# Subtracting a constant from x on ScalarE instead of GpSimd, with another set of due times, in a four-layer graph attention kernel

## The chip, the cores and the metric

The kernel runs on one core of a Trainium2 chip. A core has TensorE for matrix products (its weight loads are listed apart as PEld), VectorE (DVE), ScalarE (ACT), GpSimd (POOL) and SyncE (SP). Each engine takes its own instructions strictly in the order in which they were written for it, and waits at each until what it needs has arrived. SP and POOL issue most of the DMA transfers. The metric is the device time of one execution in microseconds.

## The reference

x has the shape 8 x 2048 x 128 (batch, node, feature), and adj is a symmetric 2048 x 2048 matrix of 0 and 1 with the diagonal set. Four layers follow each other, each of the form x = x + layer(relu(layernorm(x)), adj):

- Layers 0, 1 and 3 are graph attention. With Wh = h W and two scores per node s1 and s2, the weights are softmax over j of leaky_relu(s1[i] + s2[j]), limited to neighbours. Layer 0 ends in elu, layer 1 in nothing. Layer 3 scales its input per node, normalizes Wh a second time, adds Wh as a residual and ends in elu.
- Layer 2 has four heads of 32 features: softmax over j of leaky_relu(x[i] . x[j]), limited to neighbours, applied to x itself.

elu(v) is v for positive v, and exp(v) - 1 otherwise, so elu(v) = min(exp(v), 1) + max(v, 0) - 1. The two elus of a batch element bring a -1 each. A layernorm doesn't change when a constant is added to the whole of its input, so the kernel takes 2 from x once, ahead of the layers, and leaves out both -1.

## The kernel before

**Staging.** `fast` holds the whole adjacency matrix in on-chip memory as bytes (`edge`) and up to four batch elements of x (`X[b]`, 128 partitions x 16 blocks x 128 features, so 2048 numbers per partition). A unit is one layer of one batch element: class `Gat` for layers 0, 1 and 3, `Heads` for layer 2.

**Work of a unit.** `rows_made` normalizes x: VectorE takes statistics (L460), GpSimd raises the variance to -0.5 (`moments_power`, L111), and ScalarE makes the normalized rows (L527; for layer 3 also L534). TensorE transposes them (L558) and projects them (L588). A `Gat` then runs 32 tokens, 16 for each half of the target nodes. For a token, VectorE makes a 128 x 1024 mask of weights (L756), and TensorE multiplies it with the projected rows in eight products (L765, two instructions each). `out` divides, applies elu and adds the result to x, partly by DMA from the POOL queue (L834). A `Heads` runs 64 beats, 16 per head: TensorE makes scores (L1051), ScalarE exponentials of 128 x 1024 (L1058, two per beat), VectorE masks them and sums (L1064), TensorE weighs the values with them (L1073).

**Start.** 16 adjacency rows of 1 MB each are loaded from the SP queue (L368), and VectorE turns each into bytes (L371). `symmetry` and `verdict` establish with TensorE products and ScalarE squares (L385, L389, L395) that the matrix is symmetric, so that `fast` may be used; another path, `general`, follows only if not.

**The subtraction.** `load_x` loads a batch element from the SP queue (L423). For b > 0 its completion isn't given to the layers, but to `less_two` (L430), which adds -2 to the whole of `X[b]` on GpSimd; the statistics of layer 0 need that. For b = 0 the layers start at once, and `less_two(0, ...)` is needed only ahead of the result of layer 0 (`self.less`).

**What sets the order.** The order on the engines is planned while the program is built. Every step is an `Op` with its engine, an assumed duration, a due time, the steps it needs, and the buffers that it takes and frees. `Plan.run` moves through assumed time: of the steps that could start on an engine within WINDOW_US of the first that can, the one with the lowest due time comes next, and is written to that engine's queue. A step that takes a mask buffer (`zg`) counts as HURRY_US earlier while more than one such buffer is free. `Plan` starts with the counts of the buffers, among them `st=2, var=3, norm=3` for the statistics of a layernorm, two pairs of PSUM banks for scores and projections (`pair=(4, 6)`), three `zg` and five `z`.

Due times come from tables: TOKENS gives start and step for each half of a `Gat`, BEATS for each head of a `Heads`, LEADS how long before its start a unit begins. EARLY shifts kinds of steps: a mask's due time is its token's less EARLY["front"], and scores, exponentials, masks and weighings of layer 2 have "score", "exp", "mask" and "sums". `less_two` is due at its load's due time plus 18, and is assumed to last LESS_US, 3.0. The load is assumed to take 0.8 on its queue and 17 more until it has landed. Due times are ranks in a search, not times of the chip.

Of the kernel before, what the change touches and what calls it, by code (L numbers as in the profile page):

```python
# [8 lines left out]
F32 = mybir.dt.float32  # L9
# [5 lines left out]
AF = mybir.ActivationFunctionType  # L15
OP = mybir.AluOpType
# [4 lines left out]
P = 128  # L21
# [19 lines left out]
def adj_preln_d4(ctx: ExitStack, tc: tile.TileContext, x, adj, w0, a0, w1, a1, w3, a3,  # L41
# [17 lines left out]
    nc = tc.nc  # L59
# [8 lines left out]
    const = ctx.enter_context(tc.tile_pool(name="const", bufs=1))  # L68
# [6 lines left out]
    plus_8, minus_8 = plus_8.bitcast(F8), minus_8.bitcast(F8)  # L75
    shift = const.tile([P, 1], F32, name="shift")
    nc.vector.memset(shift, L2_SHIFT)
    neg_half = const.tile([P, NB], F32, name="neg_half")
    nc.vector.memset(neg_half, -0.5)
    edge = const.tile([P, NB, N], U8, name="edge")  # L80
# [75 lines left out]
            self.needs = [n for n in needs if n is not None]  # L156
            self.got, self.end, self.users, self.ready = {}, None, [], 0.0

    HURRY_US, WINDOW_US, BEAT_SUMS_US = 38.6, 0.138, 0.86

    EARLY = dict(front=-419.0, score=436.6, exp=-72.7, mask=-319.1, sums=-351.0)

    SINGLY = (7,)
    FIRST_ALONE = 4
    DIRECT, ROWS_TURNED, L1_ACT, L3_DMA, L3_OUT = ((0, 0), (0, 1), (7, 1), (7, 2)), True, False, True, False
    L3_PLUS, LESS_US = True, 3.0
    PLUS_US, PLUS_LAG_US, GATHER_US, GATHER_LAG_US = 1.0, 5.5, 2.2, 6.5

    class Plan:
# [11 lines left out]
        def add(self, engine, us, due, emit, needs=(), takes=(), frees=(), lag=None, tiled=False):  # L181
            op = Op(engine, us, due, emit, needs, takes, frees, self.LAG[engine] if lag is None else lag, tiled)
            self.ops.append(op)
            return op
# [56 lines left out]
    def fast(ctx):  # L241
# [12 lines left out]
        add = plan.add  # L254
# [161 lines left out]
        X, done = {}, {}  # L416

        def load_x(b, due):
            def load(op):
                X[b] = big.tile([P, NB, C], F32, tag="x", name="x", bufs=4)  # L420
                xv = x[b].rearrange("(n p) c -> p n c", p=P)
                for sl in ([slice(0, NB)] if b else [slice(q * 4, q * 4 + 4) for q in range(4)]):
                    nc.sync.dma_start(out=X[b][:, sl, :], in_=xv[:, sl, :])  # L423

            x_taken[b] = add("SP", 0.8 if b else 2.8, due, load, loaded[:] if b else (), takes=["x"], lag=17.0 if b else 3.5)
            done[b, 0] = [x_taken[b]]
            if b:
                done[b, 0] = [less_two(b, due, done[b, 0])]

        def less_two(b, due, needs):  # L430
            return add("POOL", LESS_US, due + 18.0, lambda op: nc.gpsimd.tensor_scalar(
                X[b], X[b], -2.0, None, op0=OP.add), needs)

        x_taken, behind, y_takers = {}, [], []

# [127 lines left out]
        class Gat(Unit):  # L563
            def beginning(self):
                layer = self.layer
                step = 0.2 if layer != 3 else 0.09
                rhs = {0: rhs0, 1: rhs1, 3: rhs3}[layer]
                made = self.rows_made(0.16, step)
                self.less = [less_two(0, 60.0, [m[1] for m in made])] if (self.b, layer) == (0, 0) else []
                ends, exped, self.v_ready = [], [], []  # L570
                for q in range(4):
# [177 lines left out]
            def token(self, a, due, place, last_front, last_back, first, last, gate=None):  # L749
# [11 lines left out]
                def back(op):  # L761
                    z = self.z.pop(a)
                    for i in range(HB):
# [6 lines left out]
                powers = self.powers if self.layer == 3 else self.r_made[jb // 4]  # L770
                f = add("DVE", 1.2, due - EARLY["front"], front, [last_front, r_ready, rows_in[jb], powers, gate if first else None], takes=["zg"],
                        frees=[("r", taker)] if last else [])
# [156 lines left out]
        class Heads(Unit):  # L929
# [79 lines left out]
            def beats(self, heads):  # L1009
# [4 lines left out]
                for h, (start, step) in enumerate(heads):  # L1014
                    ops = self.load(h, start - 24.0)
                    for jb in range(NB):
# [3 lines left out]
                        for c2 in range(2):  # L1020
                            score = add("PE", 0.455, due - EARLY["score"] + c2, lambda op, s=s, c2=c2: self.scores(op, s, c2),
                                        [score, ops[jb // HB], ops[2]], takes=["pair"] + ["z"] * (c2 == 0))
                            if c2 == 0:
                                z_taker = score
                            exps.append(add("ACT", 1.0, due - EARLY["exp"] + c2, lambda op, s=s, c2=c2, sc=score: self.exp(
                                op, s, c2, sc.got["pair"]), [score], frees=[("pair", score)]))
                        if jb % HB == HB - 1:
                            score.frees.append(("s", ops[jb // HB]))
                        if jb == NB - 1:
                            score.frees.append(("m", ops[4]))  # L1030
                        mask = add("DVE", 2.3, due - EARLY["mask"], lambda op, s=s: self.mask(op, s), [mask] + exps)
                        last.append((z_taker, mask))
                        self.masks.append(mask)
                        if jb % 2 or self.b in SINGLY:
                            n = len(last)
                            weigh = add("PE", BEAT_SUMS_US * n, due - EARLY["sums"], lambda op, s=s, n=n: self.weigh(op, range(s + 1 - n, s + 1)),
                                        [ready, ops[3]] + [m for _, m in last], takes=["low"] * (jb < n),
# [78 lines left out]

        GATES = {(6, 3, 0): (7, 10), (6, 3, 1): (7, 48)}
        TOKENS = {
            (1, 0, 0): (-1045.4, 4.85), (0, 1, 0): (-640.7, 2.76), (0, 1, 1): (-252.6, 5.26),
            (1, 0, 1): (550.0, 6.31), (2, 0, 0): (640.4, 1.65), (2, 0, 1): (28.7, 5.99),  # L1120
            (3, 0, 0): (595.5, 5.24), (1, 1, 0): (-448.5, 2.29), (1, 1, 1): (332.9, 2.97),
            (3, 0, 1): (532.2, 0.52), (2, 1, 0): (784.6, 2.05), (2, 1, 1): (661.4, 2.82),
            (0, 3, 0): (396.7, 5.64), (0, 3, 1): (806.2, 5.15), (3, 1, 0): (813.2, 3.88),
            (3, 1, 1): (626.5, 5.48), (4, 0, 0): (591.3, 5.35), (4, 0, 1): (1159.9, 3.82),
            (1, 3, 0): (344.0, 3.1), (1, 3, 1): (397.9, 2.03), (4, 1, 0): (753.3, 4.65),
            (4, 1, 1): (1047.7, 3.31), (5, 0, 0): (479.5, 5.62), (5, 0, 1): (203.1, 3.96),
            (2, 3, 0): (275.8, 2.82), (2, 3, 1): (1277.7, 3.76), (5, 1, 0): (1267.3, 4.61),
            (5, 1, 1): (1977.2, 2.02), (6, 0, 0): (1682.3, 4.62), (6, 0, 1): (3248.3, 1.23),
            (3, 3, 0): (1175.5, 6.08), (3, 3, 1): (3008.8, 4.11), (6, 1, 0): (2045.9, 2.48),
            (6, 1, 1): (4526.4, 1.12), (7, 0, 0): (2470.3, 4.97), (7, 0, 1): (3262.3, 5.89),  # L1130
            (7, 1, 0): (3469.2, 1.36), (7, 1, 1): (1171.1, 3.15), (4, 3, 0): (4676.8, 5.42),
            (4, 3, 1): (5085.4, 3.02), (5, 3, 0): (4390.1, 5.94), (5, 3, 1): (4885.6, 2.92),
            (6, 3, 0): (2908.7, 3.34), (6, 3, 1): (4037.1, 4.64), (7, 3, 0): (4000.6, 5.22),
            (7, 3, 1): (5814.3, 5.51),
        }
        BEATS = {
            (0, 0): (-220.15, 3.75), (0, 1): (-955.77, 16.21), (0, 2): (-787.01, 14.33),
            (0, 3): (-409.05, 11.49), (1, 0): (-2460.25, 8.82), (1, 1): (-1730.24, 5.06),
            (1, 2): (-1606.84, 2.64), (1, 3): (-953.34, 10.37), (2, 0): (-2913.87, 25.55),
            (2, 1): (-2031.19, 8.77), (2, 2): (-2016.23, 3.56), (2, 3): (-1169.09, 26.22),  # L1140
            (3, 0): (-1338.93, 12.99), (3, 1): (-767.9, 5.05), (3, 2): (-479.82, 24.71),
            (3, 3): (-27.48, 28.61), (4, 0): (-143.12, 33.04), (4, 1): (-664.45, 3.41),
            (4, 2): (334.06, 12.12), (4, 3): (242.61, 6.98), (5, 0): (826.36, 18.62),
            (5, 1): (1257.23, 30.09), (5, 2): (1720.93, 28.28), (5, 3): (2793.45, 29.54),
            (6, 0): (36.7, 6.18), (6, 1): (792.41, 2.76), (6, 2): (1584.95, 2.49),
            (6, 3): (1301.55, 25.56), (7, 0): (-8.2, 11.67), (7, 1): (679.99, 18.73),
            (7, 2): (696.97, 6.2), (7, 3): (1110.52, 5.04),
        }
        LEADS = {
            (0, 0): 213.98, (1, 0): 444.85, (0, 1): 1602.72, (2, 0): 431.88, (1, 1): 877.58,  # L1150
            (3, 0): 3092.27, (2, 1): 1432.74, (0, 3): 1030.57, (3, 1): 74.24, (4, 0): 353.64,
            (1, 3): 11.54, (4, 1): 2797.96, (5, 0): 147.39, (2, 3): 1104.42, (5, 1): 1467.02,
            (6, 0): 886.38, (3, 3): 685.98, (6, 1): 1353.96, (7, 0): 1011.38, (4, 3): 329.93,
            (7, 1): 187.82, (5, 3): 415.04, (6, 3): 2047.57, (7, 3): 660.0, (0, 2): -575.06,
            (1, 2): 1872.75, (2, 2): 1864.09, (3, 2): -603.36, (4, 2): -1021.51, (5, 2): 1002.6,
            (6, 2): -1562.71, (7, 2): 1149.25,
        }

        def planned():
# [217 lines left out]
    with ExitStack() as inner:  # L1377
        inner.enter_context(tc.manual_schedule(engines={
            mybir.EngineType.PE, mybir.EngineType.Activation, mybir.EngineType.DVE,
            mybir.EngineType.Pool, mybir.EngineType.SP}))  # L1380
        fast(inner)
# [28 lines left out]
```

## Time and profile before

| | us |
|---|---|
| median of 3 runs | 2758.52 |
| lowest and highest run | 2756.85, 2759.89 |
| the profiled execution, its own time | 2765.24 |
| its span, from the first to the last instruction | 2763.5 |
| busy: TensorE, VectorE, ScalarE, GpSimd | 2637.1, 2515.8, 1712.1, 331.5 |
| GpSimd in L431, eight times | 45.6 |
| GpSimd in L111, 39 times | 159.1 |

The mean granted TensorE clock is 0.99 of full. Busy time is the time in which an instruction of the engine was under way. In the views, a row of a group has the line in the code, the engine, the operation, the tile written and the tiles read, the shapes and the count; behind the bar come busy time, mean duration in ns, and the idle time ahead of these instructions with what ended it. A row of the waits reads "who waits <- whom: us in total, times, longest". A row of the order of time has start and duration in us; a duration with a count above x1 covers that many instructions in a row.

### The profile page before, as it was taken

How to read it: one execution, taken by the hardware profiler on the slowest of the kernel's cores; microseconds unless marked ns; L12 is line 12 of the kernel's file. 1: busy time of each engine (PE TensorE's matmuls, PEld its weight loads, DVE VectorE, ACT ScalarE, POOL GpSimd, SP SyncE). 2: the span in 40 equal slices, each digit the busy share in tenths (PEclk: the TensorE clock that was granted, in tenths of full speed). 3: DMA queues.
4: the chain of work that ended last, by engine and by line, in shares of the span. 5: the costliest groups of instructions: out<-in, count | busy, mean ns of one | idle time of the engine just before them, and what ended most of it. 6: DMA issues, size and time to landing. Idle time of an engine off the chain costs nothing. (4 is left out here: it accounts for less than half of the span.)

```text
span 2763.5 us, 49024 instructions
## 1 busy us (share of the span) xinstructions
PE 2637.1 (95%) x20104; PEld 2024.9 (73%) x20104; DVE 2515.8 (91%) x3303; ACT 1712.1 (62%) x2769; POOL 331.5 (12%) x151
## 2 busy tenths in 40 slices
PE   7899999989999999999999999999999899999997
PEld 6799877857776776866777767777685368666687
DVE  8867989989999999898999989999999689999977
ACT  2524565667665776656857568665656956787641
POOL 4200010011001110011101111011110101011010
PEclk9999999999999999999999999999999999999999
DMA  8002323152343232332433322423234321623121
GB/s 310 16 9 65 89 62 62 32 120 42 77 108 80 61 75 54 77 77 62 95 67 62 85 55 62 96 53 83 54 71 86 59 39 32 130 54 70 35 47 33
DMA packets 216874, 196.48 MB, mean 71 GB/s; under 512 B 142896, under 2 KB 178176, under 8 KB 210496
## 3 DMA queue, kind: packets, MB, share of 16 engines
q1 hardware_dynamic: 144112, 156.46, 21.1%
q0 software_dynamic: 72112, 36.73, 10.7%
q8 instruction: 160, 2.62, 0.4%
q14 instruction: 74, 0.61, 0.1%
q10 hardware_dynamic: 416, 0.07, 0.0%
HBM read 123.03 MB, written 33.73 MB: 57 GB/s over the span
## 5 line engine op out<-in xcount | busy, mean ns | idle before, releaser
L1058 ACT ACTIVATE z<-ps,shift 128x1024 f32<-128x1024 f32 x1024 | 1121.1, 1113 | 721.4 <-PE ps L1051 715.5
L765 PEld LDWEIGHTS ps<-y,zg 128*128 128x128 f32 x12288 | 1466.8, 193 | 91.2 <-DVE zg L756 37.6
L765 PE MATMUL ps<-y,zg 128*128 128x129 f32 x12288 | 1499.2, 277 | 30.5 <-DVE zg L756 22.2
L1064 DVE SCALAR_TENSOR_TENSOR z<-z,edge 128x2048 f32<-128x2048 f32 x512 | 1170.3, 2287 | 70.4 <-ACT z L1058 67.8
L756 DVE SCALAR_TENSOR_TENSOR zg<-r,cr,edge 128x1024 f32<-128x1024 f32 x768 | 992.8, 1309 | 113.5 <-PE ps L765 97.2
L1051 PE MATMUL ps<-m,s 128*128 128x512 f32 x2048 | 717.4, 437 | 48.5 <-ACT z L1058 47.4
L1051 PEld LDWEIGHTS ps<-m,s 128*128 128x128 f32 x2048 | 314.5, 190 | 323.2 <-ACT z L1058 221.5
L1073 PE MATMUL ps<-z,v 128*32 128x512 f32 x4096 | 505.2, 605 | 3.0 <-DVE z L1064 2.8
L1073 PEld LDWEIGHTS ps<-z,v 128*32 128x32 f32 x4096 | 103.7, 109 | 238.2 <-issue 183.4
L527 ACT ACTIVATE h<-x,nmrx,rstdx 128x128 f32<-128x128 f32 x512 | 210.4, 492 | 36.9 <-DVE nmrx L116 29.9
L111 POOL TENSOR_TENSOR rstdx<-varx,neg_half 128x16 f32<-128x16 f32 x31 | 129.0, 4161 | 415.2 <-DVE varx L106 406.1
L834 POOL DMA_DIRECT2D x<-oa x40 | 35.7, 892 | 934.5 <-DVE oa L798 239.6
L1098 POOL DMA_DIRECT2D x<-o x31 | 66.0, 2128 | 582.0 <-DVE o L1093 562.2
L588 PEld LDWEIGHTS ps<-rhs,h_t 128*128 128x128 f32 x768 | 99.4, 195 | 15.7 <-DVE h_t L579 4.0
L588 PE MATMUL ps<-rhs,h_t 128*128 128x130 f32 x768 | 105.6, 282 | 3.9 <-DVE h_t L579 2.8
L460 DVE BATCH_NORM_STATS2 st<-x 128x6 f32<-128x128 f32 x496 | 106.0, 282 | 1.1 <-DMA x<-oa 1.1
L558 PE MATMUL ps<-ident,h 128*128 128x128 f32 x512 | 79.5, 278 | 5.5 <-DVE y L617 2.8
L558 PEld LDWEIGHTS ps<-ident,h 128*128 128x128 f32 x512 | 61.9, 142 | 23.0 <-ACT z L1058 6.3
L798 DVE TENSOR_TENSOR oa<-ps,rs 128x384 f32<-128x384 f32 x144 | 73.9, 513 | 5.1
L579 ACT COPY h_t<-ps 128x512 f32<-128x512 f32 x92 | 53.3, 583 | 35.4 <-PE ps L558 35.3
L804 ACT ACTIVATE oe<-oa 128x1024 f32<-128x1024 f32 x32 | 33.9, 1059 | 64.0 <-DVE oa L823 55.5
L626 ACT ACTIVATE y<-ps,y 128x128 f32<-128x128 f32 x240 | 68.4, 368 | 0.0
(128 smaller groups left out, 875.1 us busy)
## 6 DMA issues: line engine op xcount, KB each, us to landing
s<-halves SPq DMA_DIRECT2D x256, 128.0 KB, 2.7
m<-halves SPq DMA_DIRECT2D x64, 512.0 KB, 6.8
r<-row SPq DMA_DIRECT2D x42, 512.0 KB, 3.8
x<-oa POOLq DMA_DIRECT2D x40, 512.0 KB, 4.7
raw<-in_adj_dram SPq DMA_DIRECT2D x16, 1024.0 KB, 13.8
values<-h SPq DMA_DIRECT2D x32, 256.0 KB, 2.2
halves<-hi SPq DMA_DIRECT2D x128, 64.0 KB, 1.7
halves<-lo SPq DMA_DIRECT2D x128, 64.0 KB, 1.7
```

The costliest lines, as they stand in the source:

```text
L111: nc.gpsimd.tensor_tensor(out=rstd, in0=v, in1=neg_half, op=OP.pow)
L460: nc.vector.bn_stats(out=key["st"][:, n, :], in_=rows()[:, n, :])
L527: nc.scalar.activation(self.h[q][:, k, :], X[self.b][:, n, :], AF.Relu, scale=key["rstd"][:, n:n + 1], bias=key["nmr"][:, n:n + 1])
L558: nc.tensor.transpose(pk[:, k, :], self.h[q][:, k, :], ident)
L588: nc.tensor.matmul(pv[:, k, :C + 2], lhsT=self.h_t[q][:, k * P:(k + 1) * P], rhs=rhs, start=True, stop=True)
L756: nc.vector.scalar_tensor_tensor(z, self.r[half], self.cr[:, 0, jb:jb + 1], edge[:, jb, half * HN:(half + 1) * HN], op0=OP.max, op1=OP.mult)
L765: nc.tensor.matmul(ps[:, self.banks(half, place)[i // 3], k * CE:(k + 1) * CE], lhsT=z[:, i * P:(i + 1) * P], rhs=self.y[:, jb, :], start= ...
L798: nc.vector.tensor_mul(key["a"][:, i0:i1, :], pv[:, :, :C], r[:, i0:i1, None].to_broadcast([P, i1 - i0, C]))
L1051: nc.tensor.matmul(ps[:, lo + c, :], lhsT=self.S[h, jb // HB][:, at:at + P], rhs=self.M[h][:, (c2 * 2 + c) * 512:(c2 * 2 + c + 1) * 512], ...
L1058: nc.scalar.activation(self.z[s][:, c2 * HN:(c2 + 1) * HN], ps[:, lo:lo + 2, :].rearrange("p b t -> p (b t)"), AF.Exp, bias=shift)
L1064: nc.vector.scalar_tensor_tensor(self.z[s], self.z[s], 1.0, edge[:, jb, :], op0=OP.mult, op1=OP.mult, accum_out=self.den[:, h, jb:jb + 1])
L1073: nc.tensor.matmul(ps[c * HD:(c + 1) * HD, 0, :], lhsT=self.V[h][:, jb, :], rhs=z[:, c * 512:(c + 1) * 512], start=jb == 0, stop=jb == NB - 1,
```

## The change

Three things change.

- `less_two` becomes an activation on ScalarE, out = Identity(x + bias), in place, with the bias in a new tile `minus_two` of 128 x 1 that is set once at the start. It needs the same steps as before, and the same steps need it. Its due time is still that of the load plus 18.
- Its assumed duration LESS_US goes from 3.0 to 1.9.
- All numbers in HURRY_US, WINDOW_US, EARLY, TOKENS, BEATS and LEADS are others, apart from BEAT_SUMS_US. The order in which TOKENS lists the halves, GATES, the buffers and the other instructions stay.

The counting of the layernorm statistics as buffers, which the change's name also speaks of, is in the kernel before and in no line of the diff.

```diff
+    minus_two = const.tile([P, 1], F32, name="minus_two")
+    nc.vector.memset(minus_two, -2.0)
...
-    HURRY_US, WINDOW_US, BEAT_SUMS_US = 38.6, 0.138, 0.86
+    HURRY_US, WINDOW_US, BEAT_SUMS_US = 54.8, 0.148, 0.86
-    EARLY = dict(front=-419.0, score=436.6, exp=-72.7, mask=-319.1, sums=-351.0)
+    EARLY = dict(front=-488.9, score=652.2, exp=89.3, mask=-87.7, sums=-385.5)
...
-    L3_PLUS, LESS_US = True, 3.0
+    L3_PLUS, LESS_US = True, 1.9
...
         def less_two(b, due, needs):
-            return add("POOL", LESS_US, due + 18.0, lambda op: nc.gpsimd.tensor_scalar(
-                X[b], X[b], -2.0, None, op0=OP.add), needs)
+            return add("ACT", LESS_US, due + 18.0, lambda op: nc.scalar.activation(
+                X[b], X[b], AF.Identity, bias=minus_two), needs)
...
         TOKENS = {
-            (1, 0, 0): (-1045.4, 4.85), (0, 1, 0): (-640.7, 2.76), (0, 1, 1): (-252.6, 5.26),
+            (1, 0, 0): (-1862.2, 4.85), (0, 1, 0): (-1216.0, 6.8), (0, 1, 1): (-220.6, 7.44),
...
-            (6, 1, 1): (4526.4, 1.12), (7, 0, 0): (2470.3, 4.97), (7, 0, 1): (3262.3, 5.89),
+            (6, 1, 1): (4526.2, 10.07), (7, 0, 0): (2367.7, 7.52), (7, 0, 1): (2792.7, 6.45),
...
         BEATS = {
-            (0, 0): (-220.15, 3.75), (0, 1): (-955.77, 16.21), (0, 2): (-787.01, 14.33),
+            (0, 0): (-161.82, 3.21), (0, 1): (-919.72, 17.96), (0, 2): (-887.13, 24.2),
...
-            (7, 2): (696.97, 6.2), (7, 3): (1110.52, 5.04),
+            (7, 2): (1457.66, 3.08), (7, 3): (2140.19, 3.89),
...
         LEADS = {
-            (0, 0): 213.98, (1, 0): 444.85, (0, 1): 1602.72, (2, 0): 431.88, (1, 1): 877.58,
+            (0, 0): 256.75, (1, 0): 1070.77, (0, 1): 113.95, (2, 0): 1008.81, (1, 1): 1403.32,
```

## The prediction

> **What bounds the kernel now.** I read the page's header and slices first, then the group of the instruction that moves, then VectorE's order of time around each of its eight executions, then the same stretches as windows, then TensorE's waits.
>
> ```profile
> span 2763.5 us, 49024 instructions
> PE 2637.1 (95%) x20104; PEld 2024.9 (73%) x20104; DVE 2515.8 (91%) x3303; ACT 1712.1 (62%) x2769; POOL 331.5 (12%) x151
> ```
>
> TensorE is busy 95% and VectorE 91%. TensorE stands idle for 2763.5 - 2637.1 = 126.4 us. ScalarE has 1051 us free, GpSimd is nearly empty. Either of the two full engines can be the bound of a stretch, so the question is which one is late where.
>
> The instruction that moves, from its own view and from the groups:
>
> ```profile
> L431 POOL TENSOR_SCALAR x<-x x8: 5374/5707/6219, 17.6 to 1927.2; 128x2048 f32<-128x2048 f32 x8
> ...
> L431 POOL TENSOR_SCALAR x<-x 128x2048 f32<-128x2048 f32 x8 | 45.6, 5710 | 78.0 <-DMA x<-in_x_dram 72.8 <-DMA raw<-in_adj_dram 5.2
> ```
>
> 45.6 us of a free engine look harmless, and no wait names this line as its releaser. VectorE's order of time beside it says otherwise. These are rows of three stretches of it (start, duration, operation):
>
> ```profile
> 17.70 6.31 DVE L371 TENSOR_SCALAR edge<-raw 128x2048 uint8<-128x2048 int32 x1
> ...
> 54.18 1.28 DVE L756 SCALAR_TENSOR_TENSOR zg<-r,cr,edge 128x1024 f32<-128x1024 f32 x1
> 55.38 1.23 DVE L371 TENSOR_SCALAR edge<-raw 128x2048 uint8<-128x2048 int32 x1
> 56.51 18.59 DVE L756 SCALAR_TENSOR_TENSOR zg<-r,cr,edge 128x1024 f32<-128x1024 f32 x7
> ...
> 862.72 5.86 DVE L756 SCALAR_TENSOR_TENSOR zg<-r,cr,edge 128x1024 f32<-128x1024 f32 x2
> ```
>
> GpSimd runs L431 at 17.55 to 22.92, three times at 56.26 to 73.36, and at 862.14 to 868.03. In each stretch a VectorE instruction is held until GpSimd is done: an edge row takes 6.31 us (1.22 elsewhere), seven masks L756 take 18.59 us (they follow each other every 1.2, so 8.5), and a pair takes 5.86 (a pair at 391.14 took 2.47). The other three stretches show L756 at 3.87, 5.86 for two, and 4.66.
>
> Is VectorE the bound where this happens? The windows of the slices with the four later executions, and of one that matters below (columns: window, length, busy of PE, PEld, DVE, ACT, POOL with counts, clock, DMA share, GB/s):
>
> ```profile
> 828.00:897.00 69.00, 65.01 (x492) 46.90 (x484) 68.77 (x79) 38.45 (x39) 8.72 (x5) 1.00 0.35 81
> 1173.00:1242.00 69.00, 64.88 (x464) 45.70 (x464) 68.49 (x97) 40.48 (x44) 12.19 (x5) 0.98 0.37 77
> 1518.00:1587.00 69.00, 66.77 (x505) 49.62 (x506) 67.04 (x65) 38.98 (x43) 10.34 (x5) 1.00 0.40 85
> 1863.00:1932.00 69.00, 68.27 (x527) 51.88 (x529) 67.08 (x63) 39.92 (x43) 8.89 (x5) 1.00 0.41 90
> 2139.00:2208.00 69.00, 55.24 (x310) 24.38 (x310) 46.75 (x63) 63.46 (x124) 11.80 (x3) 0.95 0.32 62
> ```
>
> In the first two VectorE is full (68.77 and 68.49 of 69) while TensorE loses 3.99 and 4.12 us; in the next two TensorE loses 2.23 and 0.73. In the last row ScalarE is the bound (63.46) and TensorE loses 13.8. TensorE's waits, as far as a releaser is seen:
>
> ```profile
> PE ps L1051 <- ACT z L1058: 47.4, 89, 1.4
> PE ps L765 <- DVE zg L756: 22.2, 29, 3.3
> ```
>
> The larger is scores waiting for exponentials (34 of these 89 waits lie in 2060 to 2280), the second is tokens waiting for masks.
>
> **What the Trainium skill says.** "SBUF — State Buffer", section "Who interferes with whom": GpSimd's ports are VectorE's second pair; a VectorE instruction with two SBUF inputs, or in a two-port mode, and a GpSimd instruction that reads SBUF exclude each other for a whole instruction, and ScalarE never takes part. The trace agrees for L371 and L756, and the one-input statistics L460 at 1214.77 keep their pace (0.87 for four) beside GpSimd. It doesn't agree for everything that GpSimd runs: the power L111 (3.83 us and more) ran at 388.63 to 393.99 and two masks beside it took 2.47, so I count no stall for it. "ScalarE: Activation LUTs", section "What ACT_TABLE_LOAD costs": an activation with a pointer bias takes about 280 ns + 0.833 ns per element, and one engine pass does the add. Identity already runs here (L534, L666) and the trace has one table load, so no further load. "Perfetto Trace Analysis", section "Identifying the Most-Contended Engine", warns that matmul busy overstates how full TensorE is; here weight loads are busy 73% against 95%, so some slack hides inside the 95%.
>
> **The change part by part**, against the profiled execution's 2765.2 us (span 2763.5 and 1.7 around it; the median of the runs is 6.7 lower).
>
> *GpSimd's subtraction removed.* Extra VectorE time: 6.31 - 1.22 = 5.1; 18.59 - 8.5 = 10.1; 5.86 - 2.47 = 3.4; 3.87 - 1.28 = 2.6; 5.86 - 2.47 = 3.4; 4.66 - 1.28 = 3.4. Sum 28.0 us. What of it is on the path:
> - Before 79 us, 15.2. VectorE is full (44.2 us busy of the 45.5 from 33.5 to 79), so the first 5.1 shift everything behind it, unless the adjacency rows then come late (the DMA share is 0.94 in the first 33.5 us): 3 to 5.1, take 4. Of the 10.1, TensorE stood idle for 1.74 + 1.32 + 1.00 = 4.1; from 79 on VectorE waits for TensorE (0.83, 0.74, 1.69 ahead of its masks), so no more than 4.1 comes through, and 2.5 if the symmetry products that filled the gaps need their own time then. Together 8.
> - The four later ones, 12.8. TensorE idled in those very stretches for 1.69 + 0.16 + 0.75 + 0 = 2.6, over their whole slices for 11.1. Low end 2.6, high end 11.1; I take 7, since VectorE is full in two of the four slices.
> Sum -15; ends -8 and -28. GpSimd's freed 45.6 us are worth nothing: its other work waits for its producers. The instruction issues no DMA, so no transfer moves with it by itself.
>
> *ScalarE's activation added.* 128x2048 isn't in the trace. L579 (128x512) takes 583 ns and L697 (128x1024) 1007: 0.83 ns per element, so 1007 + 1024 x 0.83 = 1.86, and from L804's 1059 it is 1.91; the page's price gives 1.99. Eight times 1.9 = 15.2 us on an engine with 1051 free. It is hidden where an exponential can come 1.9 us later, since two score buffers lie ahead; where ScalarE is the bound (2139 to 2208) it would count whole, but the last load of x was at 1921. The three early ones stand in a row, 5.7 us, in front of the squares L395 that free PSUM for TensorE (5.7 us of TensorE's waits are for them already). The new wait for x's load now stands in ScalarE's queue, with exponentials behind it. The loads landed 5.8 to 7.6 us after their issue (856.26 to 862.14, 1576.74 to 1584.38), the plan reckons 17.8: some 10 us of margin. Ends 0 and +15; take +2.5.
>
> *minus_two.* One memset of 128x1, 0.06 us as its neighbour L77, before anything waits: nothing.
>
> *Plan's price.* 3.0 for GpSimd was 2.7 short of the 5.7 measured, and the held VectorE was in no price; 1.9 for ScalarE agrees with my estimate. The order then fits the chip better; I give it no time of its own.
>
> *Due times, HURRY_US, WINDOW_US, EARLY.* No instruction is added, but the order on all five queues changes, DMA issues with them. What there is to win: TensorE's idle 126 us, less about 28 in the first 138 us, less 16 at the end (the last matmul ends at 2747.6), less the 2.6 counted above: 80 us. Half of it is the upper end, 40. It can also lose: a second stretch as 2139 to 2208 costs 14. I take an eighth, -9.5. No row prices this; it is the weakest term.
>
> Sum -15 + 2.5 - 9.5 = -22: 2765.2 - 22 = 2743.2, and with the median's 6.7 below it 2736.5, say 2737. Its own range, from -12 to -34, is 2725 to 2747.
>
> **The rivals.**
> - *Hidden gain.* TensorE is the bound nearly everywhere, VectorE's freed time only lengthens its own waits (97 us for TensorE's zg buffers), and the new order brings nothing: -8 + 2.5, some 2753 (2747 to 2753). For it: 117 such waits. Against: the full VectorE slices.
> - *Search wins more.* Half of the 80 us goes and the stall too: -15 + 2.5 - 32, about 2714 (2695 to 2725). For it: one ScalarE-bound stretch alone loses 24.5 us of TensorE between 2070 and 2277. Against: that much idle time is spread over short waits.
> - *Slower: ScalarE-bound stretches spread.* Where the new order leaves beats of layer 2 without tokens beside them, TensorE loses 13.8 us per 69, 0.2 us per us. The other terms are -12.5, so it decides beyond 63 us more of such stretch, and is plain at 100 (+7.5): about 2766. For it: all beats and tokens got new times. Against: in EARLY the masks of layer 2 move 301 ahead of the tokens' as a whole (231 earlier, 70 later), which makes no block by itself.
> - *No change*, a gain and a loss of some ten us each: 2753 to 2764.
> - *The change doesn't do what it says:* counting the statistics as buffers (st, var, norm) is in the kernel before and in no line of the diff, so that part does nothing.
>
> **How the numbers follow.** 0.2% of the median, 5.5 us, is about what a measurement of this kernel tells from no change. Forecast 0.47, search wins more 0.20, hidden gain 0.17, no change 0.07, slower 0.09. Faster: 0.47 + 0.20 + 0.17 = 0.84; same 0.07; slower 0.09. The range leaves out a tenth on each side: half of the large gains lie below 2705, most of the slower case lies above 2761.
>
> **What would show it.** Right: no L431 on GpSimd; eight 128x2048 activations of 1.9 to 2.0 us on ScalarE; no L756 above 1.35 us and no L371 above 1.3; VectorE busy near 2488; the first token's matmuls before 31 us (33.53 now); TensorE idle 100 to 110. Wrong: L756 still long beside GpSimd's power; the activation waiting for x's load with exponentials behind it; or more slices like 2139 to 2208, with TensorE's waits for L1058 well above 47 us.

## The result, and the profile after

| | us |
|---|---|
| kernel before, median of 5 runs | 2758.51 |
| changed kernel, median of 5 runs (2732.09 to 2743.12) | 2740.24 |
| ratio, with its 95% interval | 0.9929 (0.9912 to 0.9946) |
| as a difference of 2758.5 | -19.6 (-24.3 to -14.9) |
| forecast | 2737, -22 (range 2705 to 2761) |

The changed kernel is faster by about 20 us, close to the forecast and inside the range of 2725 to 2747 that the prediction gives its sum. That it came out so close is in part luck. The experiments below bring nearly the whole gain from the engine, which the prediction put at -12.5 with ScalarE's share in it, and next to nothing from the due times, which it put at -9.5; the two errors cancel.

The header of the page after (busy time of each engine and its share of the span):

```profile
span 2734.7 us, 49017 instructions
PE 2624.4 (96%) x20104; PEld 2017.2 (74%) x20104; DVE 2489.3 (91%) x3304; ACT 1728.7 (63%) x2777; POOL 284.4 (10%) x143
```

VectorE is busy 26.5 us less (2515.8 - 2489.3), for the same work. ScalarE is busy 16.6 us more, GpSimd 47.1 less. TensorE is idle for 2734.7 - 2624.4 = 110.3 us, against 126.4.

The moved instruction, from its own view and from the groups:

```profile
L433 ACT ACTIVATE x<-x,minus_two x8: 1989/1994/2013, 18.6 to 1931.9; 128x2048 f32<-128x2048 f32 x8
...
L433 ACT ACTIVATE x<-x,minus_two 128x2048 f32<-128x2048 f32 x8 | 15.8, 1995 | 0.0
```

1.99 us each and no idle time ahead of it: the load of x had always landed when ScalarE came to it. The price of the Trainium skill, "ScalarE: Activation LUTs", section "What ACT_TABLE_LOAD costs" (280 ns + 0.833 ns per element, 1.99), agrees with the 1.989 to 2.013 us measured. My 1.86 to 1.91, drawn out from shorter activations, was 4 to 7% low.

The mask's own view, with minimum, median and maximum of its duration in ns, and VectorE's order of time where seven masks took 18.59 us before:

```profile
L758 DVE SCALAR_TENSOR_TENSOR zg<-r,cr,edge x768: 1198/1279/1287, 29.4 to 2714.6; 128x1024 f32<-128x1024 f32 x192
```

```profile
54.09 1.23 DVE L373 TENSOR_SCALAR edge<-raw 128x2048 uint8<-128x2048 int32 x1 [0.19 <-DMA raw<-in_adj_dram]
55.23 4.87 DVE L758 SCALAR_TENSOR_TENSOR zg<-r,cr,edge 128x1024 f32<-128x1024 f32 x4
60.61 1.28 DVE L758 SCALAR_TENSOR_TENSOR zg<-r,cr,edge 128x1024 f32<-128x1024 f32 x1 [0.51 <-PE ps L767]
```

No mask is above 1.29 us, of 768. Four take 4.87, and then VectorE already waits for TensorE. The first token's products start at 30.76 (33.53 before). As the prediction allowed, adjacency rows now come late for VectorE: its waits in the first 80 us, of which the largest is

```profile
DVE edge L373 <- DMA raw<-in_adj_dram: 6.2, 6, 2.1
```

against 1.1 us before. TensorE's largest waits, which answer to those shown before (47.4 and 22.2):

```profile
PE ps L1053 <- ACT z L1060: 44.5, 87, 1.4
PE ps L767 <- DVE zg L758: 10.2, 16, 2.3
```

Waits for masks fell by 12 us, waits for exponentials hardly. And the windows of the same slices:

```profile
828.00:897.00 69.00, 66.93 (x504) 47.74 (x508) 66.00 (x89) 46.06 (x67) 8.07 (x4) 1.00 0.46 74
1173.00:1242.00 69.00, 64.16 (x425) 39.15 (x427) 68.68 (x107) 49.01 (x51) 13.49 (x5) 0.98 0.48 92
1518.00:1587.00 69.00, 65.94 (x483) 46.97 (x482) 67.42 (x86) 44.24 (x48) 4.82 (x4) 1.00 0.47 92
1863.00:1932.00 69.00, 68.79 (x534) 52.85 (x537) 65.78 (x69) 39.43 (x44) 3.93 (x3) 1.00 0.43 85
2139.00:2208.00 69.00, 57.06 (x326) 30.66 (x327) 47.17 (x53) 57.89 (x103) 3.27 (x2) 0.95 0.34 58
```

A slice no longer holds the same work, so only its kind is to be compared. The last row still has TensorE idle for 11.9 of 69 us, and the slice ahead of it, 2070 to 2139, for 10.1. The whole stretch from 2070 to 2277 that the prediction named costs TensorE 22.0 us, against 24.5 before. The stretch where ScalarE is the bound was not searched away.

### The profile page after: what moved, and what is told of

It is laid out like the page before. It is cut to its first block, busy times and chain, and to the rows that moved or that the text cites. A ratio compares the mean times of both kernels' runs of the same rounds, so it can differ in the third digit from the quotient of the medians.

```text
span 2734.7 us, 49017 instructions
## 1 busy us (share of the span) xinstructions
PE 2624.4 (96%) x20104; PEld 2017.2 (74%) x20104; DVE 2489.3 (91%) x3304; ACT 1728.7 (63%) x2777; POOL 284.4 (10%) x143
## 5 line engine op out<-in xcount | busy, mean ns | idle before, releaser
L758 DVE SCALAR_TENSOR_TENSOR zg<-r,cr,edge 128x1024 f32<-128x1024 f32 x768 | 969.7, 1278 | 101.3 <-PE ps L767 87.7
L529 ACT ACTIVATE h<-x,nmrx,rstdx 128x128 f32<-128x128 f32 x512 | 210.5, 491 | 33.6 <-DVE nmrx L118 26.5
L113 POOL TENSOR_TENSOR rstdx<-varx,neg_half 128x16 f32<-128x16 f32 x31 | 130.1, 4197 | 570.1 <-DVE varx L108 561.0
```

The lines of the kernel that those rows point to most:

```text
L113: nc.gpsimd.tensor_tensor(out=rstd, in0=v, in1=neg_half, op=OP.pow)
L529: nc.scalar.activation(self.h[q][:, k, :], X[self.b][:, n, :], AF.Relu, scale=key["rstd"][:, n:n + 1], bias=key["nmr"][:, n:n + 1])
L758: nc.vector.scalar_tensor_tensor(z, self.r[half], self.cr[:, 0, jb:jb + 1], edge[:, jb, half * HN:(half + 1) * HN], op0=OP.max, op1=OP.mult)
```

## The experiments

All of them are timed against the kernel before, with runs of both in turn; a difference in us is (1 - ratio) x 2758.5. "Own order" means that every queue of an engine holds the instructions in the same order as in the kernel named, save for the subtraction itself. That is possible because the plan fixes the order, and a step can be planned for one engine and written to another. The traces agree: the kernel before and the old order on ScalarE run the same 20104 products on TensorE and the same instructions on every other engine, each engine in the same order, with the subtraction and the setting of constants left aside. Where ScalarE subtracts, `minus_two` is set as in the changed kernel; the cuts below leave that out.

### Engine and order apart

Four kernels: each of the two orders with the subtraction on the other engine, and each without it.

```diff
  # 1: tables before; planned as before, written to ScalarE
             return add("POOL", LESS_US, due + 18.0, lambda op: nc.scalar.activation(
                 X[b], X[b], AF.Identity, bias=minus_two), needs)
  # 2: tables after; planned as after, written to GpSimd
             return add("ACT", LESS_US, due + 18.0, lambda op: nc.gpsimd.tensor_scalar(
                 X[b], X[b], -2.0, None, op0=OP.add), needs)
  # 3 and 4: tables before, tables after; nothing written
             return add("POOL", LESS_US, due + 18.0,
                 lambda op: None, needs)
```

> The kernel before with its own tables and so its own order on every queue; only the eight subtractions run as activations on ScalarE, at the place in ScalarE's queue where the plan put them among the others. Theory of the prediction (the held VectorE was worth 15 us, ScalarE's work costs 2.5): 2746 us, ratio 0.9955, no mask L756 above 1.35 us. Rival 'the new order is the whole gain': 2756 to 2759. Rival 'the engine is the whole gain': 2740. If the new wait for x's load stands in ScalarE's way, above 2760.

> The changed kernel with its tables and its order on every queue; only the eight subtractions run on GpSimd again. Theory of the prediction: the stalls come back, 12.5 us above the changed kernel, 2752 (ratio 0.998), with masks of 3.5 to 4.7 us beside GpSimd. Rival 'the new order is the whole gain': 2740 to 2743. Rival 'the engine is the whole gain': 2758.

> The kernel before in its own order, with the eight subtractions left out altogether (the 2 stays in x, so the output is off by it). It shows what the subtraction costs at most. Theory of the prediction: 2743 to 2744, 2.5 us below the first kernel of this set, which is ScalarE's share. Rival 'VectorE's held time is absorbed by waits': 2756. Rival 'ScalarE's share is large': 10 us or more below the first kernel.

> The changed kernel in its own order with the eight activations left out altogether (the 2 stays in x, so the output is off by it). Theory of the prediction: ScalarE's work costs 2.5 us, so 2737 to 2738. Rival 'ScalarE's work is hidden wholly': 2740. Rival 'it costs what it lasts': 2725.

| subtraction | order before | order after |
|---|---|---|
| on GpSimd | 0 (the kernel before) | 0.9990 (0.9982 to 0.9998), -2.8 us |
| on ScalarE | 0.9932 (0.9918 to 0.9946), -18.8 us | 0.9929 (0.9912 to 0.9946), -19.6 us |
| left out | 0.9932 (0.9917 to 0.9947), -18.8 us | 0.9915 (0.9900 to 0.9930), -23.4 us |

The engine alone, in the old order, brings the whole gain. The order alone, on GpSimd, brings 2.8 us. The rival "the new order is the whole gain" is out; "the engine is the whole gain" is nearly right. My own expectations for these two, 2746 and 2752, were both missed by 5 us in its favour (medians 2741.32 and 2756.67). The granted clock is no rival for it: in the mean it was 0.9917 in the runs of the old order on ScalarE and 0.9909 in the 19 runs of the kernel before beside them, and among those 19 a clock higher by 0.001 goes with a time 1.6 us shorter, so some 1 us of the 18.8 may be the clock's. The masks say the same. First the old order on ScalarE, then the new order on GpSimd:

```profile
L431 ACT ACTIVATE x<-x,minus_two x8: 1991/1994/2013, 19.9 to 1926.9; 128x2048 f32<-128x2048 f32 x8
...
L756 DVE SCALAR_TENSOR_TENSOR zg<-r,cr,edge x768: 1202/1279/1287, 30.5 to 2722.0; 128x1024 f32<-128x1024 f32 x192
```

```profile
L433 POOL TENSOR_SCALAR x<-x x8: 5372/5780/7597, 17.2 to 1942.7; 128x2048 f32<-128x2048 f32 x8
...
L758 DVE SCALAR_TENSOR_TENSOR zg<-r,cr,edge x768: 1198/1279/4670, 31.8 to 2741.1; 128x1024 f32<-128x1024 f32 x192
```

The longest mask goes with the engine, not with the order: 1287 ns against 4670. Leaving the subtraction out on top gains nothing in the old order (0.9932 twice, each known to some 4 us either way), so what the subtraction had cost was, within that, its being on GpSimd.

Since the old order on ScalarE has the instructions of the kernel before in the same order, the same instruction can be followed through both traces. These are starts, in us, of the last reciprocal (L797, 128x2) of some halves, and how much earlier it comes on ScalarE:

| before | old order on ScalarE | earlier by | what lies between this row and the one above |
|---|---|---|---|
| 122.55 | 114.80 | 7.8 | the four early subtractions |
| 828.11 | 821.13 | 7.0 | no subtraction |
| 889.64 | 880.62 | 9.0 | that of batch element 4 |
| 1247.67 | 1236.32 | 11.4 | 5 |
| 1601.99 | 1587.44 | 14.6 | 6 |
| 1948.44 | 1932.04 | 16.4 | 7 |
| 2110.86 | 2094.44 | 16.4 | no subtraction |
| 2273.01 | 2251.75 | 21.3 | no subtraction |
| 2748.99 | 2727.63 | 21.4 | no subtraction |

A staircase: the gain comes where a subtraction was, and stays in between, but for 0.8 us lost between the first two rows. The step of 4.9 at 2273 has no subtraction in it; 2.2 of it is one row of scores that landed later in the trace of before (a wait of 4.75 against 2.58). The profiled execution of before was 6.7 us above its median, and I take that step as part of it; that is not shown.

### The early and the late subtractions

```diff
             return add("POOL", LESS_US, due + 18.0, lambda op: nc.scalar.activation(X[b], X[b], AF.Identity, bias=minus_two)
                 if b < 4 else nc.gpsimd.tensor_scalar(X[b], X[b], -2.0, None, op0=OP.add), needs)
  # the mirror: b > 3
```

> The kernel before in its own order; the subtractions of batch elements 0 to 3 (before 75 us) run on ScalarE, those of 4 to 7 stay on GpSimd. Theory: gains before 79 us come through whole, since TensorE is the bound behind them: 7.8 us, as the same divisions came earlier in the trace of the first kernel, so 2752 (ratio 0.997), and the later four hold the other 10. Rival 'the early gain is absorbed later, at the first stretch where VectorE waits': 2757 to 2759. Rival 'the start is the whole gain': 2742.

> The mirror of the fifth kernel: the kernel before in its own order, the subtractions of batch elements 0 to 3 stay on GpSimd, those of 4 to 7 run on ScalarE. Theory 'the parts add up': all eight gave 18.3 and the first four 5.5 (by the ratio), so the later four give 12.8, 2746 (ratio 0.9954), about what they held VectorE for. Theory of the prediction's sum: 7 us, 2751. Rival 'only together': the early gain and the late gain overlap, so the later four alone give 15 or more, 2743.

The early four alone: 0.9980 (0.9973 to 0.9987), -5.5 us (-7.4 to -3.6). The late four alone: 0.9971 (0.9961 to 0.9981), -8.0 us (-10.8 to -5.2). Both matter, so the rivals "the start is the whole gain" and "only together" in their plain forms are out. Their sum is 13.5 us, and all eight together gave 18.8 (14.9 to 22.6). Whether the two halves help each other or the intervals only happen to lie so isn't settled: from the limits, the sum is between 8.8 and 18.2. The late four alone didn't reach the 12.8 that I expected of them; their median of 2750.83 is what the prediction's sum had for them. In its one trace, the kernel with the early four on ScalarE is 7.4 us ahead of the kernel before at 122, 5.5 at 828 and 6.3 at the end, so in these traces part of the early gain is lost again later.

### Cut into pieces on GpSimd

```diff
             return add("POOL", LESS_US, due + 18.0, lambda op: [nc.gpsimd.tensor_scalar(
                 X[b][:, n, :], X[b][:, n, :], -2.0, None, op0=OP.add) for n in range(NB)], needs)
```

> The kernel before in its own order, each subtraction on GpSimd cut into 16 instructions of 128x128. Theory 'an instruction of GpSimd holds VectorE for its own length only': VectorE gets in after each piece, no mask above 2.0 us, but the masks beside it are still slower; part of the stall goes, 2746 to 2755. Rival 'GpSimd holds VectorE for all the time that it works on x': 2759 or more, with masks of 3.5 us and above. Rival 'short pieces hold nothing, as the power doesn't': 2741 and masks of 1.28.

0.9969 (0.9957 to 0.9981), -8.6 us: about half of the gain, with the subtraction still on GpSimd. From the views of the two lines and from the groups:

```profile
L431 POOL TENSOR_SCALAR x<-x x128: 520/526/2663, 11.3 to 1939.2; 128x128 f32<-128x128 f32 x128
...
L756 DVE SCALAR_TENSOR_TENSOR zg<-r,cr,edge x768: 1202/1280/1311, 27.4 to 2732.8; 128x1024 f32<-128x1024 f32 x192
...
L431 POOL TENSOR_SCALAR x<-x 128x128 f32<-128x128 f32 x128 | 120.3, 967 | 73.6 <-DMA x<-in_x_dram 73.6
```

The time was as the theory had it, the masks were not: I expected them slowed, and none is above 1.31 us. GpSimd pays instead. A piece takes 0.53 us in the median and up to 2.66, and the eight subtractions take 120.3 us where they took 45.6. So VectorE is not held for all the time that GpSimd works on x, and the long masks come from its doing that work in one long instruction. That the engine with the shorter instructions is the one that is held fits both kernels; no third length was tried.

Why the gain is only half can be read from the trace. By the same starts as in the staircase, the kernel with pieces is 0.4 us ahead of the kernel before at 122, where the old order on ScalarE was 7.8 ahead. From 828 to 1948 it gains 8.3, where that gained 9.4. So the pieces keep most of the gain of the late four and lose that of the early ones. At the start 48 pieces stand in a row in GpSimd's queue, and the power that follows the statistics stands behind them. VectorE waits for the power, and TensorE for the mask behind that:

```profile
56.72 33.34 POOL L431 TENSOR_SCALAR x<-x 128x128 f32<-128x128 f32 x48 [29.50 <-DMA x<-in_x_dram]
90.03 9.75 POOL L111 TENSOR_TENSOR rstdx<-varx,neg_half 128x16 f32<-128x16 f32 x3
...
93.00 0.19 DVE L116 SCALAR_TENSOR_TENSOR nmrx<-varx,rstdx 128x16 f32<-128x16 f32 x1 [4.58 <-POOL rstdx L111]
...
95.22 3.81 PE L765 MATMUL ps<-y,zg 128*128 128x129 f32 x16 [8.90 <-DVE zg L756]
```

In the old order on ScalarE that power started at 81.37, and the same products waited 1.68.

### ScalarE's share

```diff
-    nc.vector.memset(minus_two, -2.0)
+    nc.vector.memset(minus_two, -1.0)
...
             return add("ACT", LESS_US, due + 18.0, lambda op: [nc.scalar.activation(
                 X[b], X[b], AF.Identity, bias=minus_two) for k in range(2)], needs)
```

> The changed kernel in its own order, each activation done twice with -1 instead of once with -2: 16 us more of ScalarE at the same places. Theory (leaving the activations out gave 3.4 us of 16): 2743 to 2744. Rival 'hidden wholly': 2740. Rival 'it counts for what it lasts': 2756.

0.9935 (0.9922 to 0.9949), -17.9 us (-21.5 to -14.1), median 2739.93. ScalarE is busy 15.1 us more than in the changed kernel, and the time is the same within the intervals, where the rival "hidden wholly" had 2740. In the new order, left out, once and twice stand at -23.4, -19.6 and -17.9. That is a slope of about 3 us for 16 us of ScalarE, but each has an interval of some 4 us on both sides, and in the old order once and left out don't differ. So the share is between nothing and some 3 us; "it counts for what it lasts" is out.

### The due times

> The change without its due times: less_two planned and run on ScalarE with a price of 1.9, all tables, EARLY, HURRY_US and WINDOW_US as before. Theory after the first four kernels (the due times bring 1 us at most): 2738 to 2744. Rival 'the old due times don't suit the moved step, and the search made that good': 2747 to 2755.

```diff
-    L3_PLUS, LESS_US = True, 3.0
+    L3_PLUS, LESS_US = True, 1.9
...
-            return add("POOL", LESS_US, due + 18.0, lambda op: nc.gpsimd.tensor_scalar(
-                X[b], X[b], -2.0, None, op0=OP.add), needs)
+            return add("ACT", LESS_US, due + 18.0, lambda op: nc.scalar.activation(
+                X[b], X[b], AF.Identity, bias=minus_two), needs)
```

0.9969 (0.9956 to 0.9981), -8.6 us. My theory fell, and the rival holds: with the old tables, planning the step on ScalarE at 1.9 gives away 10 of the 18.8 us that the same step brings in the old order. The step now takes ScalarE's time in the plan, and the plan's other choices shift with it. The planned engine and the assumed duration were changed together, so which of the two does it isn't known. TensorE's waits show the kind of loss, for the old order on ScalarE and for the replanned one:

```profile
PE ps L1051 <- ACT z L1058: 47.3, 87, 1.4
```

```profile
PE ps L1051 <- ACT z L1058: 56.5, 96, 2.3
```

That is 9.2 us more waiting for exponentials, and 9.6 us of the row lie between 2290 and 2380, where the old order on ScalarE has no wait of scores for exponentials. The two spans differ by 9.6 us (2751.6 and 2742.0). So the new due times didn't improve on the old order by much; they made good what replanning with the old ones had lost. To see how much is left of it, the changed kernel was timed again:

> The changed kernel once more, beside the ninth kernel and the same runs of the kernel before. If its gain is the 18 to 19 us of the first measurement: 2738 to 2742. It settles by how much the due times differ from the old order with the activation (ratio 0.9932 there): theory, by no more than 0.002.

0.9925 (0.9912 to 0.9939), -20.7 us, median 2738.10. With the first measurement, the changed kernel stands 1 to 2 us below the old order on ScalarE (0.9932), and the intervals of both reach over that.

## Why the prediction was right, and where it was not

**VectorE held by GpSimd: the mechanism right, the size somewhat small.** This was the step that the forecast rested on. It said -15, with 8 from the start and 7 from the four later ones. In the old order the engine alone brought -18.8 (-22.6 to -14.9), with ScalarE's share in it, so 15 lies just inside the interval. Taken alone, the halves measured -5.5 and -8.0, near the 8 and 7; in the staircase they are 7.8 and 9.4. The ceiling for the start was well reasoned: of 15.2 us of held VectorE only half came through. VectorE waits for TensorE from 79 us on, and the adjacency rows are late once VectorE is not (waits of 5.5 us in the old order on ScalarE, 1.1 before). For the late four I took the middle of 2.6 and 11.1. In the staircase the steps are 2.0, 2.4, 3.2 and 1.8, which is 9.4 of the 12.8 that VectorE was held for (3.4, 2.6, 3.4, 3.4), although TensorE's own idle time beside them was only 2.6 in all. So the idle time right beside a held instruction was too low a measure: where VectorE was busy for 97 to 100% of a slice, about three quarters of what it lost showed up later, by the staircase.

One reading of the lines was wrong in part. I wrote that a VectorE instruction is held until GpSimd is done. That is so for the edge row, which ends 1.08 us after L431. The seven long masks all end 0.65 us ahead of it, so they were let go before. The last of them, and the subtraction beside it:

```profile
1928.06 4.66 DVE L756 SCALAR_TENSOR_TENSOR zg<-r,cr,edge 128x1024 f32<-128x1024 f32 x1
...
1927.15 6.22 POOL L431 TENSOR_SCALAR x<-x 128x2048 f32<-128x2048 f32 x1 [12.45 <-DMA x<-in_x_dram]
```

The exclusion for a whole instruction that the prediction cites thus fits the row and not the masks. The powers that hold no mask last from 2.9 us, not from 3.83.

**ScalarE's share, +2.5: not contradicted, not confirmed.** 0 to some 3 us. The wait for the load of x that now stands in ScalarE's queue cost nothing: 0.0 idle ahead of L433.

**Due times, -9.5: the step that failed.** "I take an eighth" of the idle time was a guess without a row (an eighth of 80 is 10), and against the old order the new one brings 1 to 3 us: -2.8 with GpSimd, about -1 to -2 with ScalarE. The stretch that I named as one to win, 2070 to 2277, still costs TensorE 22.0 of the 24.5 us.

**Plan's price, "no time of its own": wrong.** Writing the step to another engine's plan with the old tables cost 10 us. Together with the term above: +10 for the replanning and -11 to -12 for the new due times (from -8.6 to -19.6 and -20.7), where I had 0 and -9.5. That -11 to -12 lies near -9.5 is luck: the reason was another one, and the net of the two was near zero.

So the sum of -22 came out near -20 because the engine brought 6 us more than I put it at (18.8 against 15 less 2.5), and the order 7 to 9 us less. Two sums beside it were not what they claim: the high end of 28 for the stall is all the time that VectorE was held, where my own ceilings add up to 20.3 (5.1 + 4.1 + 11.1), and in "search wins more" half of the 80 us is 40, not 32.

**The marks.** Seen: eight activations of 1.99, no long mask, VectorE at 2489.3 (2488 expected), the first token at 30.76 (before 31), no wait of ScalarE for x. Missed: one edge row took 1.68 us (no row above 1.3 was expected; it ran at 13.65, while GpSimd issued the small DMAs of L298 and L299 from 13.13 to 15.45), TensorE's idle is 110.3, at the edge of 100 to 110. Of the rivals, "hidden gain" took too small a share of the stall, and "search wins more" and "slower" didn't come.

## What to carry to other kernels

An engine that is nearly empty can still cost: look, in the order of time of the busiest engine, at what its instructions do beside each of the idle engine's, since no wait names the one that holds it. When one step of a planned order moves, time it first in the old order with only that step written elsewhere; this tells the step's worth from the plan's, and here the plan could have eaten half of the gain. A long instruction on the holding engine can also be cut, which here freed VectorE, but it made that job 2.6 times as long, and what stood behind it in the same queue came late.

## What the runs showed of the hardware that was not expected

- One GpSimd instruction of 128x2048 (5.37 us or more) holds a VectorE mask for up to 3.4 us (4.67 instead of 1.28) and an edge row for 5.1 (6.31 instead of 1.22). Each of the eight holds one VectorE instruction and no more. Sixteen of 128x128 hold a mask by no more than 0.03, and are themselves stretched from 0.53 to 0.97 us in the mean.
- All seven held masks of the kernel before, and all five of the new order on GpSimd, end 0.65 us before the GpSimd instruction beside them; the edge row ends 1.08 after it, in both. If each then took its usual time, a mask was let go about 1.93 us before GpSimd's end and the row about 0.14 before it (an estimate from these durations).
- The power L113 (L111 before) on GpSimd lasts some 4 us, and no mask of 768 in the changed kernel is above 1.29 us with 39 of these powers in the run; 54 of the masks ran beside one. So it isn't the length of an instruction on GpSimd alone that holds VectorE. The runs don't tell what in it decides; the power reads 128x16 elements of two tiles, the subtraction 128x2048 of one, and they are different operations. Whether it is the reading or the writing of x that holds VectorE was not tried.
